# Attention scores of the plain dimensions as four float32r products in 64 rows, two heads side by side, with the maxima in a product of their own

## The chip, the core and the metric

The kernel runs on one core of one Trainium2 chip. The metric is the device time of one execution in microseconds, lower is better; a figure for a kernel is the median of its runs. Engines are named as in the profile: PE is TensorE (PEld its weight loads), DVE VectorE, ACT ScalarE, POOL GpSimd, SP the engine that here only issues DMAs.

## The reference, cut to what matters

The reference is a network of two layers over 1024 tokens of 256 numbers, each block with a layer norm ahead of it and a residual sum behind it. In order: attention a (16 heads of 16 dimensions), a ternary feed-forward block, attention b (a gated delta rule), the feed-forward block again, attention c (as a, with other weights), a mixture of experts, attention d (causal, 16 plain dimensions and 64 rotated ones for each head), the mixture of experts again. The change concerns the scores in a, c and d:

```python
# a and c, for each head; a adds a bonus per key
scores = q @ k.T * scale                # 16 dimensions
out = softmax(scores) @ v
# d
scores = (einsum('bhtd,bhsd->bhts', q, k) + einsum('bhtd,bsd->bhts', qr, kr)) * scale
scores = where(causal, scores, -inf)
out = softmax(scores) @ v
```

All is float32.

## The kernel before

**Blocks.** Everything stays on the chip: `x` (1024 tokens in eight tiles of 128) lives in SBUF and each block adds to it. `HALF` is 512 tokens, `P` 128, `GH` 4 heads make a group, `HT` 4 tiles a half, `NT` 8 tiles.

**The class `Stack` (L365 to L472)** holds q and k of the plain dimensions so that one product gives a nearly exact score. `make` takes 128 rows (8 heads by 16 dimensions) of q or k for 512 tokens from PSUM, copies them to `full`, and splits them into three bfloat16 pieces: ACT casts (L402), the engine named in `eng` subtracts (L403), ACT casts the rest (L405), POOL subtracts (L406). SP writes the pieces to a DRAM tile `dpc` (L407). `fetch` (L415) reads them back in another arrangement: for each head 96 rows, which are the six pairs of pieces that matter (`RUNS`), 16 dimensions each, in three DMAs. So a head's scores are one bfloat16 product over 96 rows. In the q block rows 96 to 98 hold the three pieces of the negated row maximum, and in the k block ones (L400), so that the transposed scores come out with the maximum already taken off, in a product over 99 rows (`rows`, L445).

**`attend` (L172 to L363)** runs with its order written out by hand. A unit is a group of four heads for one half of the queries; there are eight. A step `n` does three things, each for another unit or key tile:

- `look`: scores of one query tile against up to 512 keys, two heads into one double PSUM bank (tag `s`, two of them), and DVE's negated `reduce_max` over it (L227); in d DVE adds the causal mask first (L224).
- `weigh`, ten steps later (`LAG`): the same scores transposed, one key tile against up to 512 queries. Each head has a PSUM bank of tag `st`, of which there are three; ACT writes the exponential to `pr` (L252, in a with a bias L254). In d POOL cuts the diagonal block.
- `gather`, two steps after that: the sums over keys, four heads in four column strips of 32 into one bank (tag `o`, one of it), float32 (L279).

Within a step the order on PE is: two heads' looks and two heads' weights, the gather, then the same for the other two heads. `products` (L262) issues the matmuls: part by part, and within a part the two looks and then the two weights. In a and c `parts` is `[stack.rows]`, in d `[wide, stack.rows]`, where `wide` is the float32 product of the 64 rotated dimensions, heads in rows 0 to 63 and 64 to 127 by turns. In the first ten steps there are looks alone (four heads in one go), in the last ten weights alone (two heads in a double `s` bank, two in `st` banks), and at the end two steps of gathers.

When a unit's looks end, `settle` (L291) takes the smaller of the two negated maxima and `Stack.begin` (L454) splits it in three pieces on POOL; a step later `Stack.place` (L465) turns them with a product against the identity into a bank of tag `st`, DVE copies them (L470) and SP moves them into rows 96 to 98 of the q block (L472). When a unit's gathers end, `close` (L302) divides by the sums: DVE transposes (L311), POOL multiplies. `early`, `chores` and `last` are lists of further work put into given steps: the blocks of q and k still to be made, values, the output projection (L492, also in a bank of tag `st`), the next block's norm, loads.

**`plain`** (L500) prepares a and c, **`attn_d`** (L577) d: there the staging tiles of `make` are the later `pr` buffers and a spare tile. Outside `attend` a planner orders the instructions by costs and due times.

[...]

## Time and profile before

| what | value |
| --- | --- |
| median of three runs | 1514.51 us (1509.39 to 1522.26) |
| profiled execution | 1517.28 us, its span 1515.6 us |
| granted TensorE clock, mean | 0.957 |
| PE, PEld, DVE, ACT, POOL busy | 93%, 45%, 54%, 43%, 25% |
| attention a | 0 to 274 us |
| attention c | 615 to 862 us |
| attention d | 1013 to 1357 us |
| between them, and after d | feed-forward, b, feed-forward; mixture of experts |

The span is the time from the first to the last instruction of the profiled execution. In the profile's groups a line stands for all instructions of one source line with the same operands: number, busy time, mean time of one, and the idle time of the engine ahead of them with what ended it. L267 is the one matmul of `products`; its groups differ by the names `s` (looks) and `st` (weights; `stt` in a double bank), and by bf16 (`rows`) or f32 (`wide`). Matmul times hold the latency of the pipe, so the distance from one start to the next says more than a mean. A float32 product shows as two records, each of two passes; a float32r product shows as one record with the form f32. In the timeline consecutive instructions of one group are merged: start, time from the first start to the last end, count. The windows give, for a stretch, its length and then busy time and number of instructions for PE, PEld, DVE, ACT and POOL, the granted clock, the DMA engines' share and GB/s.

### The profile page before, as it was taken

Reading aid. Unit: us, or ns where it says so; the run is one execution under the profiler, and the core shown is the slowest. Engines: PE = TensorE matmul, PEld = TensorE weight load, DVE = VectorE, ACT = ScalarE, POOL = GpSimd, SP = SyncE. Lnnn points to the kernel's source line nnn. Section 1 sums busy time; section 2 is a strip of 40 time slices with the busy share of each in tenths; the row PEclk is TensorE's granted clock in tenths of the full one; section 3 lists DMA queues with packets and bytes.
Section 4 is the critical chain, followed back from the end, with each engine's and each line's share of the span. In section 5 each row is a group of like instructions: output and inputs, shape, how many; then the busy total and the mean of one; then the engine's idle time right before and its main releaser. Section 6 shows DMA issues by size and latency. Waiting matters only on the chain.

```text
span 1515.6 us, 18778 instructions
## 1 busy us (share of the span) xinstructions
PE 1402.0 (93%) x7250; PEld 679.8 (45%) x7250; DVE 824.8 (54%) x1357; ACT 645.1 (43%) x1165; POOL 373.0 (25%) x574
## 2 busy tenths in 40 slices
PE   5899989988799999899989999998899999899999
PEld 3222322665456888423332434553333334444454
DVE  4788768545673564688867231236545555523111
ACT  3488668445542235367756531112233333233100
POOL 1211100430458004211100124332221222230533
PEclk9799989998899999989999989999999999998999
DMA  5412002000012110531300100003310100000000
GB/s 157 111 33 87 2 1 71 0 1 0 9 34 53 28 40 1 140 82 30 105 15 1 61 1 0 0 2 109 81 33 0 32 2 2 1 1 1 0 14 14
DMA packets 51000, 51.40 MB, mean 34 GB/s; under 512 B 25116, under 2 KB 45212, under 8 KB 49436
## 3 DMA queue, kind: packets, MB, share of 16 engines
q1 hardware_dynamic: 42944, 35.82, 9.1%
q10 hardware_dynamic: 7968, 14.40, 3.8%
q8 instruction: 57, 0.93, 0.3%
q14 instruction: 31, 0.25, 0.1%
HBM read 37.06 MB, written 12.85 MB: 33 GB/s over the span
## 4 chain that ended last, share of the span: by engine, by line
PE 79%; DVE 11%; issue 3%; ACT 3%; DMA 2%; POOL 1%; ACTq 0%; SPq 0%; DVEq 0%; POOLq 0%
PE s L267 14%; PE st L267 11%; PE o L279 9%; DVE mx L227 4%; PE pu L1385 3%; PE po L1563 3%; PE pj L155 3%; PE pu L1507 3%; PE pg L1385 3%; PE pg L1507 3%; PE po L155 2%; PE py L1545 2%; PE ln L759 2%; PE pg L155 2%; PE pu L155 2%
## 5 line engine op out<-in xcount | busy, mean ns | idle before, releaser
L227 DVE TENSOR_REDUCE mx<-s 128x2 f32<-128x1024 f32 (+3 forms) x352 | 395.5, 1146 | 119.3 <-PE s L267 117.0
L252 ACT ACTIVATE pr<-st 128x512 f32<-128x512 f32 (+3 forms) x408 | 201.2, 556 | 214.7 <-PE st L267 211.5
L267 PE MATMUL s<-k,q 96*128 96x512 bf16 (+3 forms) x704 | 209.8, 386 | 14.3 <-DVE mx L227 12.7
L267 PE MATMUL st<-q,k 99*128 99x512 bf16 (+3 forms) x644 | 195.3, 377 | 5.7 <-ACT pr L254 2.4
L279 PE MATMUL o<-pr,V 128*32 128x512 f32 (+3 forms) x1408 | 182.0, 590 | 0.0
L254 ACT ACTIVATE pr<-st,bonus 128x512 f32<-128x512 f32 x236 | 145.3, 688 | 41.5 <-PE st L267 41.4
L267 PEld LDWEIGHTS <-q 96*128 96x128 bf16 x704 | 53.1, 99 | 203.6 <-issue 178.1
L267 PEld LDWEIGHTS <-k 99*128 99x128 bf16 x704 | 67.3, 100 | 93.0 <-issue 23.5
L1519 DVE TENSOR_TENSOR sl<-sl,pg 128x512 f32<-128x512 f32 (+1 forms) x48 | 30.8, 642 | 132.3 <-PE pg L1507 112.3
L267 PE MATMUL s<-kr,qr 64*128 64x512 f32 (+3 forms) x384 | 91.8, 540 | 4.2 <-DVE mx L227 2.2
L1514 ACT ACTIVATE sl<-pu 128x512 f32<-128x512 f32 (+1 forms) x48 | 26.8, 561 | 144.4 <-PE pu L1507 141.1
L1521 POOL TENSOR_TENSOR hT<-sl,mask 128x512 f32<-128x512 f32 x40 | 50.6, 1266 | 147.7 <-DVE sl L1519 98.1
L267 PE MATMUL st<-qr,kr 64*128 64x512 f32 (+3 forms) x344 | 78.1, 506 | 0.1
L313 POOL TENSOR_TENSOR raw<-raw,rc 128x512 f32<-128x512 f32 x24 | 25.1, 1047 | 187.9 <-DVE rc L312 187.9
L258 POOL TENSOR_SCALAR_AFFINE_SELECT pr<-pr 128x128 f32<-128x128 f32 x128 | 35.4, 292 | 124.8 <-ACT pr L252 123.6
L224 DVE TENSOR_TENSOR s<-s,squares 128x256 f32<-128x256 f32 x64 | 27.6, 431 | 69.8 <-PE s L267 69.6
L279 PEld LDWEIGHTS o<-pr,V 128*32 128x32 f32 x1408 | 29.1, 109 | 77.9 <-issue 73.1
L91 POOL TENSOR_TENSOR hT<-sl,hT 128x512 fp32r<-128x512 f32 x32 | 41.1, 1293 | 85.2 <-ACT hT L90 85.2
L267 PEld LDWEIGHTS s<-kr,qr 64*128 64x128 f32 x384 | 31.6, 186 | 51.7 <-issue 21.2
L135 PE MATMUL ln<-squares,xn 128*128 128x128 f32 x112 | 22.7, 303 | 34.1 <-DVE xn L132 31.5
L1385 PE MATMUL pu<-xT,m_up 128*128 128x512 f32 (+1 forms) x112 | 50.0, 597 | 0.0
L267 PEld LDWEIGHTS st<-qr,kr 64*128 64x128 f32 x344 | 36.9, 192 | 23.9 <-issue 14.1
(355 smaller groups left out, 2161.1 us busy)
## 6 DMA issues: line engine op xcount, KB each, us to landing
dpc<-pc SPq DMA_DIRECT2D x16, 384.0 KB
k<-dpc SPq DMA_DIRECT2D x12, 192.0 KB
k<-dpc ACTq DMA_DIRECT2D x6, 384.0 KB
q<-dpc SPq DMA_DIRECT2D x6, 384.0 KB
dpc<-spare SPq DMA_DIRECT2D x5, 384.0 KB
q<-dpc SPq DMA_DIRECT2D x12, 128.0 KB
k<-dpc SPq DMA_DIRECT2D x12, 128.0 KB
k<-dpc ACTq DMA_DIRECT2D x6, 256.0 KB
```

What stands on the lines that cost most here:

```text
L91: eng.tensor_tensor(dst[:, 1], src, dst[:, 0].bitcast(F32), ALU.subtract)
L155: pe.matmul(ps, lhsT=a, rhs=b, start=(n == 0), stop=(n == len(pairs) - 1))
L227: dve.reduce_max(maxima[u][:, pair : pair + 2, t % HT, c // HALF], ps[:, :, :size], axis=AX.X, negate=True)
L252: act.activation(pr[:, js, :wide], ps, AF.Exp)
L254: act.activation(pr[:, js, :wide], ps, AF.Exp, bias=bias[:, kt : kt + 1])
L258: pool.affine_select(block, block, [[1, P]], ALU.is_ge, 0.0, base=0, channel_multiplier=-1)
L267: pe.matmul(dst, lhsT=a, rhs=b, start=(i == 0), stop=(i == len(parts) - 1))
L279: pe.matmul(sums[u][32 * j : 32 * j + 32, c0:c1], lhsT=V[:, kt, 17 * (g * GH + j) : 17 * (g * GH + j) + 32], rhs=weights[m][0][:, j, c0 - ...
L1385: pe.matmul(ps[rs, own], lhsT=wt[wn][:, k, es], rhs=xT[:, k, tokens], start=(k == 0), stop=False)
L1507: pe.matmul(ps[rs, own], lhsT=wt[wn][:, es], rhs=z[hf, m, j][:, tokens.start - cols.start : tokens.stop - cols.start], start=False, stop=T ...
L1521: pool.tensor_tensor(hT[rs, own], sl[rs, own], masks[3 + j][rs, tokens], ALU.mult)
L1563: pe.matmul(po[b], lhsT=l, rhs=r, start=(n == 0), stop=False)
```

## The change

Each of q and k is split into two float32r pieces instead of three bfloat16 ones (`halve`), and a head's rows are 64 instead of 96: four products of pieces (q0k0, q0k1, q1k0, q1k1) of 16 dimensions each. Even heads of a group lie in rows 0 to 63 of the block, odd heads in rows 64 to 127; `across` orders the weights' columns to match. `fetch` makes four DMAs, of 32 rows each, that repeat pieces as the four products need.

The maxima leave the q and k blocks. They go to a tile `top` (bfloat16, cleared once), rows 0 to 11 and 64 to 75 (three pieces by four heads, twice), and a constant `pick16` selects the head: `shift` is a part of its own, a bfloat16 product over 64 rows that is issued only for the transposed scores, after all products of the part `rows`. `place` therefore issues two DMAs.

```diff
--- before.py
+++ after.py
@@ -262,9 +262,11 @@
         def products(todo):
             for i, part in enumerate(parts):
                 for dst, h, qs, ks, turn in todo:
+                    if part(h, qs, ks, turn) is None:
+                        continue
                     q, k = part(h, qs, ks, turn)
                     a, b = (k, q) if turn else (q, k)
-                    pe.matmul(dst, lhsT=a, rhs=b, start=(i == 0), stop=(i == len(parts) - 1))
+                    pe.matmul(dst, lhsT=a, rhs=b, start=(i == 0), stop=(i == len(parts) - 2 + turn))
 
         def gather(m, c0, c1):
 
@@ -369,9 +371,9 @@
 
 
 
-        RUNS = ((0, 0, 48), (48, 0, 32), (80, 0, 16)), ((0, 0, 48), (48, 16, 32), (80, 32, 16))
-        ROWS = 96
+
         BH = 8
+        ROWS = 64
 
         def __init__(self, p, dp, space=None):
 
@@ -381,30 +383,33 @@
                 self.stage = self.p.__enter__()
             self.of = {}
             self.kept = {}
+            self.tops = {}
+            self.pick = load(p, "pick16", w["pick16"], [P, 2, P])
+            self.ring = []
+            self.extend(p.tile([P, HALF], BF16, tag=f"top{n}", name="top") for n in range(1 if space else 2))
+
+        def extend(self, more):
+
+            for t in more:
+                pool.memset(t, 0.0)
+                self.ring.append(t)
 
         def make(self, n, b, hf, ps, use, eng):
 
             if self.space is None:
                 full = self.stage.tile([P, HALF], F32, tag="full", name="full", bufs=2)
-                rest = self.stage.tile([P, HALF], F32, tag="rest", name="rest", bufs=1)
-                pc = self.stage.tile([P, 3, HALF], BF16, tag="pc", name="pc", bufs=2)
+                pc = self.stage.tile([P, 2, HALF], F32R, tag="pc", name="pc", bufs=2)
             else:
                 flat = self.space()
-                full, rest = flat[:, :HALF], flat[:, HALF : 2 * HALF]
-                pc = flat[:, 2 * HALF : 2 * HALF + 3 * HALF // 2].bitcast(BF16).rearrange("p (c n) -> p c n", c=3)
-            d = self.dp.tile([3 * P, HALF], BF16, tag=f"d{n}{b}{hf}", name="dpc")
+                full = flat[:, :HALF]
+                pc = flat[:, HALF : 3 * HALF].bitcast(F32R).rearrange("p (c n) -> p c n", c=2)
+            d = self.dp.tile([2 * P, HALF], F32, tag=f"d{n}{b}{hf}", name="dpc")
             use(b, full, ps)
             name = "k" if n else "q"
-            st = self.of[n, b, hf] = self.blocks.tile([P, self.BH, HALF], BF16, tag=name, name=name, bufs=3 + n)
-            if n:
-                nc.sync.dma_start(out=st[self.ROWS : self.ROWS + 3], in_=w["ones16"])
-            first, last = (2, 0) if n else (0, 2)
-            act.copy(pc[:, first], full)
-            eng.tensor_tensor(rest, full, pc[:, first], ALU.subtract)
+            self.of[n, b, hf] = self.blocks.tile([P, self.BH // 2, HALF], F32R, tag=name, name=name, bufs=3 + n)
+            halve(eng, pc, full)
             yield
-            act.copy(pc[:, 1], rest)
-            pool.tensor_tensor(pc[:, last], rest, pc[:, 1], ALU.subtract)
-            nc.sync.dma_start(out=d.rearrange("(c p) n -> p c n", p=P), in_=pc)
+            nc.sync.dma_start(out=d.rearrange("(c p) n -> p c n", p=P), in_=pc.bitcast(F32))
             self.kept[n, b, hf] = d
             yield
 
@@ -414,9 +419,17 @@
 
         def fetch(self, n, b, hf, eng, hs=slice(0, BH)):
 
-            d = self.kept[n, b, hf].rearrange("(r h) n -> r h n", h=self.BH)
-            for dst, src, m in self.RUNS[n]:
-                eng.dma_start(out=self.of[n, b, hf][dst : dst + m, hs], in_=d[src : src + m, hs])
+
+            d = self.kept[n, b, hf].rearrange("(c s r j) n -> s c r j n", c=2, s=2, j=self.BH // 2)
+            js = slice(hs.start // 2, hs.stop // 2)
+            for side in range(2):
+                for m in range(2):
+                    src = d[side, m, None] if n == 0 else d[side]
+                    r = side * self.ROWS + m * self.ROWS // 2
+                    eng.dma_start(
+                        out=self.of[n, b, hf].bitcast(F32)[r : r + self.ROWS // 2, js],
+                        in_=src[:, :, js].to_broadcast([2, 16, js.stop - js.start, HALF]),
+                    )
 
         def rest(self, early, make, hf, later):
 
@@ -443,13 +456,21 @@
                 at(last + 4 + n, work)
 
         def rows(self, h, qs, ks, turn):
-            m = self.ROWS + 3 if turn else self.ROWS
+            r = slice(h % 2 * self.ROWS, (h % 2 + 1) * self.ROWS)
             return tuple(
                 self.of[n, h // self.BH, c.start // HALF][
-                    :m, h % self.BH, c.start % HALF : c.start % HALF + c.stop - c.start
+                    r, h % self.BH // 2, c.start % HALF : c.start % HALF + c.stop - c.start
                 ]
                 for n, c in ((0, qs), (1, ks))
             )
+
+        def shift(self, h, qs, ks, turn):
+
+            if not turn:
+                return None
+            r = slice(h % 2 * self.ROWS, (h % 2 + 1) * self.ROWS)
+            c0 = qs.start % HALF
+            return self.tops[h // GH, qs.start // HALF][r, c0 : c0 + qs.stop - qs.start], self.pick[r, h % GH // 2, :]
 
         def begin(self, ap, g, hf, nm):
 
@@ -468,8 +489,9 @@
             pe.matmul(pt, lhsT=self.kept.pop((g, hf)).rearrange("p c n -> p (c n)"), rhs=ident16, start=True, stop=True)
             nmT = ap.tile([3 * n, P], BF16, tag="nmT", name="nmT")
             dve.tensor_copy(nmT, pt)
-            j0 = g % 2 * GH
-            nc.sync.dma_start(out=self.of[0, g // 2, hf][self.ROWS : self.ROWS + 3, j0 : j0 + GH, :], in_=nmT)
+            top = self.tops[g, hf] = self.ring[len(self.tops) % len(self.ring)]
+            for side in range(2):
+                nc.sync.dma_start(out=top[side * self.ROWS : side * self.ROWS + 3 * GH], in_=nmT)
 
     def value_tile(p):
 
@@ -530,7 +552,7 @@
         early = {}
         stack.rest(early, make, 0, later)
         out_tile = partial(out_project, wt[letter + "_wo"], wt[letter + "_bo"])
-        attend(a2, pp, [stack.rows], stack, V, False, bias, early, out_tile, after, last)
+        attend(a2, pp, [stack.rows, stack.shift], stack, V, False, bias, early, out_tile, after, last)
 
     def attn_a(wt, norm, after, later, last):
 
@@ -687,9 +709,11 @@
                 for j in range(2):
                     early[(g + 2) * NT + LAG - NT + j].append(partial(turned_rows, g, 0, j))
             spare[0] = xpool.tile([P, KC * S], F32, tag="xT", name="spare")
+            more = [wt[n].rearrange("p k n -> p (k n)").bitcast(BF16) for n in ("d_wqd", "d_wkvd")]
+            early[0].append(lambda: stack.extend(more))
             stack.rest(early, make, 1, [])
             attend(
-                a2, pp, [wide, stack.rows], stack, V, True, None, early, partial(out_project, wo, None), after,
+                a2, pp, [wide, stack.rows, stack.shift], stack, V, True, None, early, partial(out_project, wo, None), after,
                 deque(),
             )
             ctx_d.close()
@@ -1732,7 +1756,9 @@
         "m_order": np.tile(np.arange(EXP, 0, -1), (P, 1)),
     }
     c32 = {k: np.ascontiguousarray(v, dtype=np.float32) for k, v in c32.items()}
-    c16 = {"ones16": np.ones((3, 8 * HALF), ml_dtypes.bfloat16)}
+    side, row = np.divmod(np.arange(P)[:, None, None], 64)
+    pick = (row < 12) & (row % 4 == 2 * np.arange(2)[:, None] + side) & (np.arange(P) >= 0)
+    c16 = {"pick16": pick.astype(ml_dtypes.bfloat16)}
     return {**c32, **c16, "m_spread": np.stack([np.asarray(s, np.float32) for s in spread], 1).astype(ml_dtypes.bfloat16)}
 
 
@@ -1747,7 +1773,7 @@
     a, b, c, d, m = "L0_attn_a_", "L0_attn_b_", "L1_attn_a_", "L1_attn_b_", "L1_ffn_"
     def across(wt):
 
-        return wt.reshape(-1, 2, NH // 2, 16).transpose(0, 1, 3, 2).reshape(-1, NH * 16)
+        return wt.reshape(-1, 2, NH // 4, 2, 16).transpose(0, 1, 3, 4, 2).reshape(-1, NH * 16)
 
     w = {"x": i[a + "hidden_states"].reshape(S, D)}
     for n in "qk":
```

## The prediction

> **What bounds the kernel now.** I read the head of the page first, then the attention's matmul groups, then the timeline of a few steps, and last the windows that show three steps at a time.
>
> ```profile
> span 1515.6 us, 18778 instructions
> PE 1402.0 (93%) x7250; PEld 679.8 (45%) x7250; DVE 824.8 (54%) x1357; ACT 645.1 (43%) x1165; POOL 373.0 (25%) x574
> ...
> L267 PE MATMUL s<-k,q 96*128 96x512 bf16 (+3 forms) x704 | 209.8, 386 | 14.3 <-DVE mx L227 12.7
> L267 PE MATMUL st<-q,k 99*128 99x512 bf16 (+3 forms) x644 | 195.3, 377 | 5.7 <-ACT pr L254 2.4
> ```
>
> PE looks full, and the products that the change touches (`s` and `st` of L267, bf16) are 405 of its 1402 us. That share says little: what counts is what ends one step of `attend`. One whole step of attention a, PE and then ACT:
>
> ```profile
> 150.64 0.60 PE L267 MATMUL st<-q,k 99*128 99x512 bf16 x2
> 151.08 0.59 PE L267 MATMUL s<-k,q 96*128 96x512 bf16 x2
> 151.51 0.66 PE L267 MATMUL st<-q,k 99*128 99x512 bf16 x2
> 152.10 1.06 PE L279 MATMUL o<-pr,V 128*32 128x512 f32 x8
> 153.10 0.39 PE L267 MATMUL s<-k,q 96*128 96x512 bf16 x1
> ...
> 151.06 2.42 ACT L254 ACTIVATE pr<-st,bonus 128x512 f32<-128x512 f32 x4 [0.48 <-PE st L267]
> 153.96 0.69 ACT L254 ACTIVATE pr<-st,bonus 128x512 f32<-128x512 f32 x1 [0.48 <-PE st L267]
> ```
>
> Call a step's four transposed products st1, st2 (before the gather, L279) and st3, st4 (after it), and their exponentials e1 to e4. They share three PSUM banks in turn, so st2 can't start before e3 of the step before has read its bank. The pair at 151.51 takes 0.66 where the pair at 150.64 takes 0.60: its second product came late. The loop: e3 starts at 151.06 and takes 0.69; st2 starts 0.04 later; 0.31 until the gather (0.22 of product, 0.09 of change of tile shape); gather 1.00; two s 0.44; st3 to the start of its exponential 0.42 (150.64 to 151.06). Sum 2.90, and the gathers stand 2.90 apart. Two things confirm it. In a step where `place` takes one of the banks, the loop runs through e4, one exponential later (0.58): 3.48 is what these steps take. In attention c the exponentials take 0.60 instead of 0.69 and stand 0.49 apart: the loop is 2.81, PE's own sum 2.83 and observed 2.83; with `place` 2.81+0.49=3.30, observed 3.30. So a and c sit on a round trip through PE and ACT that is as long as PE's own work. Three steps each of a, c, and attention d:
>
> ```profile
> 72.61:81.31 8.70, 8.70 (x49) 2.56 (x48) 6.84 (x6) 8.16 (x15) 2.31 (x2) 1.00 0.20 56
> ...
> 662.70:671.20 8.50, 8.50 (x49) 2.56 (x48) 6.81 (x6) 7.08 (x15) 2.31 (x2) 1.00 0.20 61
> 1143.75:1163.13 19.38, 19.38 (x101) 6.96 (x100) 10.27 (x16) 6.51 (x13) 2.99 (x3) 1.00 0.00 1
> ```
>
> In d (6.46 a step) ACT works 6.5 of 19.4 us: here PE's own work is the bound.
>
> **Prices of the new products.** No float32r product in 64 rows exists. Nearest are the ffn's float32r products over 128 rows, and d's float32 products in 64 rows:
>
> ```profile
> 295.97 1.07 PE L155 MATMUL pg<-xT,f_wg 128*128 128x512 f32 x4
> ...
> 286.18 0.72 PE L155 MATMUL pg<-xT,f_wg 128*128 128x512 f32 x2
> ...
> 1157.67 0.92 PE L267 MATMUL s<-kr,qr 64*128 64x384 f32 x4
> 1158.42 1.02 PE L267 MATMUL st<-qr,kr 64*128 64x512 f32 x4
> 1159.38 0.50 PE L267 MATMUL s<-k,q 96*128 96x384 bf16 x2
> ```
>
> Four float32r products take 1.07, the last 0.39 of it: 0.227 from start to start, against 0.216 in bf16. After a wait (286.18) two take 0.72, so the first spacing is 0.33: its weight load (188 ns a row, bf16 100) starts only with the product, and 0.11 of it shows. In d two heads in rows 0-63 and 64-127 run at once: four records, two passes for each head, in the time of two (1158.42 to 1159.38). I take a float32r pair at 0.23, or 0.33 after a wait or a change of shape; the shift pair (bf16, 64 rows, `pick` and `top`) at 0.22. Bounds: 0.23 if the pair overlaps and the load hides, 0.45 if the two heads follow each other. Between float32r and bf16 in one shape I take no gap: at 471.99 a 128*128 f32 follows a 128*128 bf16 after 0.22, the bare product.
>
> **Attentions a and c.** Removed per step: eight bf16 products (1.73). Added: four pairs (0.92) and two shift pairs (0.43). PE's own sum falls from 2.83 to about 2.6. But the shifts stand behind both st, and an exponential can start only after its shift. The loop afterwards: wake 0.05; st2 0.33 (it waits, so its load shows; st1 has run); second shift and change of shape 0.31; gather 1.00; s pair 0.33 (load after the change of shape); st pair 0.23; shift to exponential 0.42; exponential 0.69. Sum 3.36 in a, 3.27 in c. By the gathers' starts, 33 steps of 2.90 and 6 of 3.48 get 0.46 longer, 17.9; 33 of 2.83 and 6 of 3.30 get 0.44 longer, 17.2. Three steps with `close` (3.22 in a) go to 3.36: 0.4. If both loads hid, the loops would be 3.14 and 3.05 and these steps cost 18; if one more load showed, 8.6 more (78 x 0.11).
>
> Last ten steps (no s): the second st waits for the exponential of the first of the step before: 0.05, 0.33, 0.42, the double exponential (next start 1.00 later, 0.92 in c), 0.69 (0.60): 2.49 and 2.32 against 1.97 now, on 5 and 8 clean steps: 5.4. Steps with an output projection (4.56) are PE's own work, with more changes of shape: 0.1 by ten, 1. Together **+42**, from +24 to +50.
>
> [...]
>
> **Attention d.** The rows part is behind the wide float32 part. Now it costs a change of shape in (0.10), two s and two st in turn, a change back (0.09) and the wide load that then shows (0.11). Afterwards all parts use 64 rows. Per pair this saves 0.28 (0.30 less 0.02 for the slower float32r) plus the s term (two bf16 less one pair: 0.20 at 512 columns, 0.05 at 128); a pair with the gather behind it still pays the change, and saves 0.09 plus the s term. st gains nothing: two in turn become pair and shift. Over the 38 joint steps: 38 x 0.37 = 14.1, and the s terms by the looks' widths (128 to 512) add 11.5: 25.6. The bank loop takes part of this: at 512 columns it is 0.05+0.97+0.23+0.23+0.31+1.00+0.97+0.86+0.23+0.23+0.42+0.60=6.10 against PE's 5.98 (two pairs of 2.39, gather and change 1.09, a load 0.11), and with narrower s it falls less than PE does. I take three quarters, **-19** (bounds -13, -26), and -3 in the ten steps of looks (bounds -6, 0).
>
> **The rest.** `make` loses an ACT cast (0.62) and a POOL subtraction (1.16) in the chain before the first looks; its two pieces are a third more bytes to DRAM and back (512 for 384 KB), with a fourth fetch to issue (0.43). Later blocks stand behind DVE's reductions, 1.13 each. -1 per attention, **-3** (-6, +2). `place` issues two DMAs instead of one, 0.70 each on SP; only the second head of a pair waits for the second, and the gather covers most: **+1** (0, +8). Its DMA waits on SP for DVE's copy of `nmT`; in the looks the `dpc` writes and fetches stand behind it, and they have a step to spare. A `top` comes round after two units (three in d at first), when its shifts are long done. The `pick16` load and the clearing of `top` cost nothing: the norm and the projections hide them; uncovered, one SP issue (0.46 as b_wg's) per attention. Clock: with s pairs PE does less in the DVE-bound looks.
>
> ```profile
> 45.99:49.40 3.41, 1.99 (x9) 0.67 (x7) 2.93 (x3) 1.30 (x2) 1.40 (x2) 1.00 0.84 203
> 49.40:52.81 3.41, 2.56 (x7) 0.70 (x6) 3.41 (x4) 0.62 (x1) 0.64 (x1) 0.50 0.62 129
> ```
>
> A window with PE busy 1.99 of 3.41 precedes half clock. The looks will have more such windows, the steps of 3.36 will not (some 2.6 of work): **+2** (0, +8). [...]
>
> **Sum.** +42-19-3-3+1+2=+20, on the profiled execution's 1517.28 (span 1515.6): 1537. The median of the runs, 1514.51, is 2.8 lower, so 1535 is forecast. Differences within 1% (15 us) are about what a measurement here can't tell from none.
>
> **Rivals.** (A) The loads hide, as they do in a running stream: 78 x 0.22 in the loops and 13 x 0.11 in the last steps, 18 less: 1519, or 1516 as a median. For it: loads are issued far ahead in 295.97. Against: 286.18. (B) PE's work is the bound and the banks follow: a and c fall to DVE's 2.45 a step (two reductions of 1.22), 39 x 0.45 + 39 x 0.38 = 32 less; d the full 26+3, the start 3: 1453. It decides if the loop comes out under 2.45, that is, if st2 needn't wait for e3. For it: 93% PE, and c's ordinary steps fit PE's sum too. Against: 3.48, 3.30 and the 0.07 between a and c, which differ in ACT's work only. (C) The change doesn't do what it says: 64-row float32r pairs don't overlap. The loop gains 0.68 (s, st, shift), 57 us over 84 steps; d 38 x 1.34, 51: 1645. Against: d's float32 pairs.
>
> **Chances.** Forecast 0.60, A 0.20, B 0.14, C 0.06. Slower: nearly all of the forecast and C, 0.62; within 1%: A and the forecast's low edge, 0.22; faster: B and a little of A, 0.16. The forecast's own range, terms at their bounds but not all at once, is 1515 to 1570; with A it reaches down to 1502. B and C stay outside.
>
> **What would show it.** Gathers 3.36 apart in a, 3.27 in c, 5.8 in d's wide steps; PE waiting for ACT before st2; ACT with 0.9 idle a step; two s starts within 0.01; first spacing after a gather 0.33. Gathers at 2.45 would make the forecast wrong; at 3.1, A is right.

## The result, and the profile after

The changed kernel takes 1790.42 us (median of four runs, 1788.85 to 1792.27); the kernel before, on the same chip, 1518.38. The ratio is 1.180, with an interval from 1.173 to 1.187. The forecast was 1535 us, with a range up to 1570. The profiled execution has a span of 1787.5 us, 272 more than before. Here and below a median is of all runs of a kernel, while a ratio leaves out the few runs that were over 1.5% slower than the fastest of the same kernel.

The head of the page of the kernel after (busy time by engine), its chain by engine, and its groups for the products that the change touches. The chain is the work that ended last, followed back from the last instruction, at each step to what released it; DMA stands in it for a transfer, SPq and ACTq for the issuing of DMAs on SP and ACT, and the shares are of the span:

```profile
span 1787.5 us, 20323 instructions
PE 1444.6 (81%) x7954; PEld 752.6 (42%) x7954; DVE 824.8 (46%) x1357; ACT 640.8 (36%) x1141; POOL 351.3 (20%) x557
...
PE 63%; DMA 19%; DVE 6%; ACT 5%; issue 3%; SPq 2%; ACTq 1%; POOL 1%; DVEq 0%; POOLq 0%
...
L269 PE MATMUL s<-k,q 64*128 64x512 f32 (+3 forms) x704 | 223.0, 592 | 75.6 <-DMA k<-dpc 44.6
L269 PE MATMUL st<-q,k 64*128 64x512 f32 (+3 forms) x644 | 190.0, 420 | 56.5 <-ACT pr L254 30.0
L269 PE MATMUL st<-top,pick 64*128 64x512 bf16 (+2 forms) x544 | 151.9, 401 | 66.8 <-DMA top<-nmT 66.8
```

The chain by engine of the kernel before:

```profile
PE 79%; DVE 11%; issue 3%; ACT 3%; DMA 2%; POOL 1%; ACTq 0%; SPq 0%; DVEq 0%; POOLq 0%
```

PE is busy for 43 us more, and DMA has gone from 2% of the chain to 19%, from some 30 us to 340 in which a transfer is what the end waits for. Of the idle time ahead of the scores, 45 us end with a fetch of k and 67 with the maxima's DMA; the 30 us that end with ACT are the round trip over the banks that the prediction described. PE also runs slower: its mean granted clock is 0.889 where it was 0.957. The clock's records of both kernels hold only 1.0 and 0.5, in stretches of 3.41 us or whole multiples of it (but for the last), so (1-0.889) x 2 x 1787.5 gives 397 us at half clock, against 130 before. How much of the 272 us that alone is, no run separates. Some of the longest pieces of the chain from 30 to 175 us, in attention a, whose first gather stands at 133 (start, length, what):

```profile
30.78 16.99 DMA dpc<-pc
49.06 11.38 DMA k<-dpc
60.45 4.79 SPq L429
...
72.65 17.05 DMA dpc<-pc
93.70 24.97 DMA q<-dpc
121.21 4.63 ACTq L429
139.80 10.17 DMA dpc<-pc
152.73 22.65 DMA top<-nmT
```

`top<-nmT` moves two times 12 KB and takes 22.65 us: it isn't slow itself, it stands behind fetches (in experiment 2, where the fetches are faster, no such transfer has more than 4.94 us of the chain). SP and ACT each lose 4.6 to 4.8 us on one issue of a fetch (L429), where the prediction had 0.43. What the DMA engines do in this stretch (40 equal slices of 30 to 75 us; first the busy share of all 16 engines in tenths, then GB/s):

```profile
DMA  1117511111111111111111111111112111111111
GB/s 55 55 51 308 202 51 51 51 51 55 55 51 51 51 47 55 51 51 51 55 55 51 51 51 51 51 51 51 51 51 66 51 51 58 51 51 51 51 51 51
```

51 GB/s with a tenth of the engines busy, for nearly the whole of 45 us. In the packets of the trace a fetch comes as two streams side by side, 4096 bytes in 159 to 165 ns each, one packet behind the other: 2 x 4096 bytes in 160 ns are 51 GB/s, and two packets at a time are an eighth of 16 engines, as in the busy share (0.13 from 36 to 56 us). So a fetch of 1 MB takes 20 us, on 2 engines out of 16, while the others idle.

The steady steps are as forecast. A step of attention a of the kernel after, PE and ACT:

```profile
187.53 1.06 PE L281 MATMUL o<-pr,V 128*32 128x512 f32 x8
188.53 0.50 PE L269 MATMUL s<-k,q 64*128 64x512 f32 x2
188.87 0.40 PE L269 MATMUL st<-q,k 64*128 64x512 f32 x2
189.10 0.39 PE L269 MATMUL st<-top,pick 64*128 64x512 bf16 x2
...
189.53 2.61 ACT L254 ACTIVATE pr<-st,bonus 128x512 f32<-128x512 f32 x4 [0.78 <-PE st L269]
189.56 0.39 PE L269 MATMUL st<-q,k 64*128 64x512 f32 x1
190.27 0.50 PE L269 MATMUL st<-q,k 64*128 64x512 f32 x1 [0.31 <-ACT pr L254]
190.28 0.73 PE L269 MATMUL st<-top,pick 64*128 64x512 bf16 x2
190.93 1.07 PE L281 MATMUL o<-pr,V 128*32 128x512 f32 x8
```

Two heads of a pair run in the time of one (0.40 for x2). The second of the step's first st pair starts at 190.27 and waited for ACT; ACT idles 0.78. From gather to gather 3.40, forecast 3.36. Three steps of a and 10 us of c, by windows (length, busy time of PE, PEld, DVE, ACT, POOL, the clock, DMA share, GB/s):

```profile
180.76:190.93 10.17, 9.33 (x61) 3.37 (x60) 8.39 (x10) 7.60 (x13) 1.05 (x1) 1.00 0.01 2
921.90:931.90 10.00, 9.56 (x60) 3.52 (x60) 7.95 (x9) 6.76 (x13) 2.34 (x2) 1.00 0.16 56
```

10.17 are three steps of a; gathers in c stand 3.30 apart (forecast 3.27), in d's wide steps 5.78 to 6.05 (5.8).

By the starts of the first look, the first gather and the last gather of each attention, the span falls into these parts (us; the last two columns are two experiments below):

| part | before | after | 16-row fetches | dimensions swapped |
| --- | --- | --- | --- | --- |
| to a's first look | 32.9 | 41.5 | 30.7 | 31.6 |
| a: first look to first gather | 33.5 | 91.6 | 49.3 | 37.4 |
| a: gathers | 201.8 | 257.3 | 219.3 | 215.9 |
| to c's first look | 357.8 | 366.6 | 358.6 | 358.6 |
| c: first look to first gather | 32.2 | 89.0 | 42.5 | 38.0 |
| c: gathers | 192.9 | 248.2 | 211.7 | 215.3 |
| to d's first look | 186.7 | 183.1 | 181.8 | 183.2 |
| d: first look to first gather | 64.0 | 101.1 | 69.6 | 61.7 |
| d: gathers | 250.0 | 244.2 | 232.8 | 232.8 |
| to the end | 163.9 | 165.0 | 165.0 | 165.0 |

Of the 272 us, 152 are in the three stretches from first look to first gather. The gathers of a and c have 111 more. Most of that isn't in the steady steps: in a, two steps take 18.2 and 15.6 us, in the places where the chain has `top<-nmT` (22.65 us at 152.73 and 15.56 at 229.39).

### The profile page after: what moved, and what is told of

Read it like the earlier page. It is cut to its first block, busy times and chain, and to the rows that moved or that the text cites. A ratio compares the mean times of both kernels' runs of the same rounds, so it can differ in the third digit from the quotient of the medians.

```text
span 1787.5 us, 20323 instructions
## 1 busy us (share of the span) xinstructions
PE 1444.6 (81%) x7954; PEld 752.6 (42%) x7954; DVE 824.8 (46%) x1357; ACT 640.8 (36%) x1141; POOL 351.3 (20%) x557
## 4 chain that ended last, share of the span: by engine, by line
PE 63%; DMA 19%; DVE 6%; ACT 5%; issue 3%; SPq 2%; ACTq 1%; POOL 1%; DVEq 0%; POOLq 0%
PE st L269 12%; PE o L281 8%; PE s L269 7%; DMA dpc<-pc 5%; DMA top<-nmT 5%; DMA q<-dpc 5%; PE pu L1409 2%; PE po L1587 2%; PE pu L1531 2%; PE pg L1409 2%; PE po L155 2%; PE pg L1531 2%; PE pj L155 2%; PE py L1569 2%; SPq L429 2%
## 5 line engine op out<-in xcount | busy, mean ns | idle before, releaser
L269 PE MATMUL s<-k,q 64*128 64x512 f32 (+3 forms) x704 | 223.0, 592 | 75.6 <-DMA k<-dpc 44.6
L269 PE MATMUL st<-q,k 64*128 64x512 f32 (+3 forms) x644 | 190.0, 420 | 56.5 <-ACT pr L254 30.0
L269 PE MATMUL st<-top,pick 64*128 64x512 bf16 (+2 forms) x544 | 151.9, 401 | 66.8 <-DMA top<-nmT 66.8
L269 PEld LDWEIGHTS s<-k,q 64*128 64x128 f32 x704 | 81.8, 208 | 218.6 <-issue 96.2
L269 PEld LDWEIGHTS st<-q,k 64*128 64x128 f32 x644 | 90.1, 197 | 118.4 <-ACT pr L254 53.3
L269 PEld LDWEIGHTS <-pick 64*128 64x128 bf16 x704 | 46.5, 96 | 140.2 <-issue 137.1
L269 PE MATMUL s<-kr,qr 64*128 64x512 f32 (+3 forms) x384 | 97.5, 551 | 5.5 <-DVE mx L227 3.6
L269 PE MATMUL st<-qr,kr 64*128 64x512 f32 (+3 forms) x344 | 85.7, 516 | 0.3 <-ACT pr L252 0.3
L91 POOL TENSOR_TENSOR pc<-full,pc 128x512 fp32r<-128x512 f32 x10 | 12.7, 1274 | 237.8 <-ACT pc L90 237.8
L269 PEld LDWEIGHTS s<-kr,qr 64*128 64x128 f32 x384 | 37.2, 197 | 50.6 <-issue 20.5
```

The costliest lines, as they stand in the source:

```text
L91: eng.tensor_tensor(dst[:, 1], src, dst[:, 0].bitcast(F32), ALU.subtract)
L269: pe.matmul(dst, lhsT=a, rhs=b, start=(i == 0), stop=(i == len(parts) - 2 + turn))
```

## The experiments

**1. How many engines carry a fetch.** In the source of a changed fetch, `d[side]` broadcast to `[2, 16, heads, 512]`, the outermost dimension is 2. The first two runs issue each as two DMAs of 16 rows, in one case for all fetches, in the other for k's alone.

```diff
-                    src = d[side, m, None] if n == 0 else d[side]
-                    r = side * self.ROWS + m * self.ROWS // 2
-                    eng.dma_start(
-                        out=self.of[n, b, hf].bitcast(F32)[r : r + self.ROWS // 2, js],
-                        in_=src[:, :, js].to_broadcast([2, 16, js.stop - js.start, HALF]),
-                    )
+                    for c in range(2):
+                        r = side * self.ROWS + m * self.ROWS // 2 + c * 16
+                        eng.dma_start(
+                            out=self.of[n, b, hf].bitcast(F32)[r : r + 16, js],
+                            in_=d[side, m if n == 0 else c][:, js],
+                        )
```

> The changed kernel, with each fetch issued as eight DMAs of 16 partition rows instead of four whose source has an outermost dimension of 2. Bytes and products are the same. Theory (two engines): in the changed kernel's trace the packets of a fetch come two at a time, 4096 bytes in 159 ns, so a fetch of 1 MB is carried by 2 of 16 DMA engines and takes some 20 us, and the rest queues behind it. With 16 rows outermost the packets spread over 16 engines; a fetch takes 6 to 8 us, the waits for DMA fall from 19% of the chain to some 2%, and the time falls to what the prediction's other terms give, 1535, and some 5 more for four more issues a fetch: about 1540 (1520 to 1565). Rival (bytes: 4-byte pieces and every piece read twice from DRAM): nothing changes but the number of issues, 1780 or more. Rival (half of each: engines and bytes): 1600 to 1700. The steady loops stay: gathers 3.4 apart in attention a, 3.3 in c, 5.8 to 6.0 in d's wide steps.

> The changed kernel with only k's fetches in DMAs of 16 rows; q's keep the outermost dimension of 2. Half of the fetches are k's. Theory (two engines): a part of the excess goes with them, but the first looks need both a q and a k, and q's fetch takes 20 us by itself: the time lies between the changed kernel and the one with all fetches in 16 rows, 1600 to 1720. Rival (bytes): 1780 or more. If the time were near 1540, q's fetches would be hidden and k's alone the loss.

Measured: all fetches 1563.85 us, ratio 1.030 (1.024 to 1.035); k's alone 1704.83 in one run. So 226 of the 272 us go with the two engines, and the dose holds: with q's fetches left as they were, 71, 69 and 88 us lie between first look and first gather. DMA is down to 3% of the chain. That bytes or repeated reads were the loss is out: they are the same. Not as expected are 24 us that remain above 1540. The table has them: the stretch from first look to first gather is still 15.8, 10.3 and 5.6 us longer than before.

**2. The order of the dimensions alone.** One edit to the changed kernel: 16 outermost instead of 2. Since q's and k's rows change their order alike, the scores stay as they were. Four DMAs a fetch, same bytes.

```diff
-                    src = d[side, m, None] if n == 0 else d[side]
+                    src = d[side, m, :, None] if n == 0 else d[side].rearrange("c r j n -> r c j n")
...
-                        in_=src[:, :, js].to_broadcast([2, 16, js.stop - js.start, HALF]),
+                        in_=src[:, :, js].to_broadcast([16, 2, js.stop - js.start, HALF]),
```

> The changed kernel with one edit: in the source of a fetch the two outermost dimensions change places, 16 features by 2 pieces instead of 2 by 16 (the rows of a half side then alternate between the pieces, for q and k alike). Four DMAs a fetch, the same bytes, 32 rows each. Theory (the outermost dimension of the source sets how many DMA engines carry it, and the rest of the loss with 16-row fetches, 26 us, is their rate and number: 8192-byte packets of 974 ns to 16 neighbouring rows, against 309 ns to 128 rows, and eight issues for four): the packets spread over 16 engines, and the time comes to the prediction's own sum, 1541 (1530 to 1553), the stretch from first look to first gather within 6 us of the kernel before in each attention. Rival (the order of the dimensions doesn't matter, a DMA with a repeated or strided source is slow as such): 1780 or more. Rival (the loss of 26 us is not the fetches'): as with 16 rows, 1560 to 1570.

Measured: 1541.7 us (1540.61 to 1547.72), ratio 1.016 (1.010 to 1.022). The head of its chain, and its DMA engines in 40 slices of 36 to 56 us:

```profile
PE 79%; DVE 9%; ACT 6%; issue 4%; DMA 1%; POOL 1%; ACTq 0%; DVEq 0%; SPq 0%; POOLq 0%
...
DMA  6678765647656999999000000959999889999949
GB/s 172 221 205 229 221 213 189 197 172 238 205 139 246 328 356 414 377 377 336 33 25 29 25 25 4 246 147 295 262 246 246 197 180 180 262 229 262 197 98 262
```

Some 200 GB/s where the same four DMAs with the same bytes ran at 51. The cause of these 249 us (1790.4 less 1541.7) is settled: two dimensions in the wrong order. With 2 outermost the packets come two at a time, an eighth of 16 engines; with 16 outermost the share of all 16 is 0.6 or more in 29 of these 40 slices. What other sizes of that dimension do, this run doesn't show.

**3. What 16-row fetches lose.** In the run with 16-row fetches all 16 engines take part, yet between 56 and 75 us, where the packets of ACT's fetches take 92.5% of the engines' time, only 151 GB/s are moved. Here the pieces are written to DRAM twice, in the order of the tile's rows, and a fetch is one DMA of 128 rows.

```diff
+            to = d.rearrange("(s m c r) n -> s m c r n", s=2, m=2, c=2)
+            for side in range(2):
+                for copy in range(2):
+                    out = to[side, :, copy] if n == 0 else to[side, copy]
+                    nc.sync.dma_start(out=out.rearrange("c r n -> r c n"), in_=pc.bitcast(F32)[...])
...
+            d = self.kept[n, b, hf].rearrange("(p j) n -> p j n", j=self.BH // 2)
+            eng.dma_start(out=self.of[n, b, hf].bitcast(F32)[:, js], in_=d[:, js])
```

> The changed kernel, with the pieces written to DRAM twice, in the order of the tile's rows (four writes of 256 KB instead of one of 512 KB), so that a fetch is one DMA of 128 partition rows instead of eight of 16. Theory (what 16-row fetches still lose against the prediction, from the first look to the first gather 15.8, 10.3 and 5.6 us in a, c and d, is the time to issue eight DMAs a fetch, 0.46 to 0.56 each on SP and ACT): these stretches fall back to within 4 us of the kernel before each, and the time by 15 to 28 us to 1542 (1530 to 1552). Rival (bytes): twice the bytes written, so the stretches get longer and the time is 1565 or more. Rival (the wait is for the maxima's way through POOL, PE, DVE and DMA): no change, 1558 to 1568.

Measured: 1557.19 us, ratio 1.026 (1.020 to 1.031): 15 less was the least expected, and 7 came. The stretches did fall, to 37.3, 37.2 and 66.1 us, within 5.0 of the kernel before. But the parts ahead of the first looks grew by 6.7, 4.8 and 4.5 us against 16-row fetches. The chain says why, by line: with 16-row fetches from 14 to 50 us, then with ordered writes from 20 to 80.

```profile
by line: SPq L429 38.3%; PE pv L155 19.2%; DMA dpc<-pc 17.5%; PE pj L155 15.0%; issue 5.1%; ACT full L580 2.2%; ACT xT L73 2.1%; PE ln L135 1.9%; ACT pc L90 1.7%; DVE pc L91 1.4%; DVE xT L71 1.2%; DVE xn L132 0.9%; DVE V L512 0.4%; SPq L412
...
by line: DVE mx L227 23.2%; PE pj L155 15.8%; SPq L416 10.3%; DMA k<-dpc 9.4%; PE st L269 8.8%; PE s L269 8.6%; DMA top<-nmT 7.4%; DMA dpc<-pc 7.2%; ACT pr L254 3.5%; PE o L281 2.6%; issue 1.6%; DVE pc L91 1.2%; ACT pc L90 1.0%; DVE nmT L49
```

In the first, the end waits for SP to issue fetches (L429), as the theory had it. In the second that is gone; now SP's issues of the writes (L416, eight of 0.61 to 1.24 ahead of the first look) are on the chain, so the gain is real (12.0, 5.3 and 3.5, together 20.8), and its price, 16, eats three quarters of it. Swapping the dimensions has the gain without the price. Beside the number there is the rate. The DMA engines while fetches run, to 16 rows in 56 to 75 us and to 128 rows in 60 to 75:

```profile
DMA  9997949291974989996979969595959596969696
GB/s 121 121 155 86 190 52 224 35 224 17 190 86 48 155 280 435 479 280 77 188 77 128 148 86 190 69 207 69 207 69 207 69 173 86 190 86 190 86 190 86
...
DMA  9999979659689896510963899996000000000000
GB/s 388 410 410 306 295 164 202 120 153 208 235 322 388 360 464 243 192 55 29 224 131 109 350 415 437 415 437 284 22 0 0 0 0 0 0 0 0 0 0 0
```

In the right half of the first pair, where ACT's fetches go to 16 rows each, the share is 0.9 and 0.5 or 0.6 by turns at 190 and 86, or 207 and 69, GB/s: 138 in the mean. Fetches to 128 rows: 388 to 437. In the packets, 8192 bytes take 974 ns (median, 58 to 80 us) when they go to 16 neighbouring rows and 309 when they go to 128. So here the rate rose with the rows that a transfer reaches: 138 GB/s for 16, 207 for 32 (experiment 2, the mean of the slices from 48 to 56 us), 388 to 437 for 128. What makes it so no run shows.

**4. The round trip over three banks.** With 16-row fetches, the gather is cut into halves, one after each pair.

```diff
                         if v is not None:
-                            if pair == 0:
-                                gather(v, 0, HALF)
+                            gather(v, pair * HALF // 4, (pair + 2) * HALF // 4)
```

> The changed kernel with 16-row fetches, and the gather of a step cut into two halves of 256 columns, one after the first pair of scores and one after the second. Nothing else moves. Theory (round trip over three PSUM banks): each half of the gather lies in another lap of the banks, so a lap has 0.50 less: 3.36-0.50=2.86 in a, 2.77 in c, though PE has two more changes of shape (0.2) a step; over 78 steps some 38 us less than with 16-row fetches alone, about 1525 (1515 to 1540). Rival (PE's own work is the bound in these loops): the gathers stand 3.5 apart or more and the time is 10 us or more above that of 16-row fetches alone.

Measured: 1551.79 us, ratio 1.022 (1.016 to 1.028), 12 less than with the gather whole. PE of this kernel in one half step of a, and ACT:

```profile
88.82 0.50 PE L269 MATMUL s<-k,q 64*128 64x512 f32 x2
89.16 0.40 PE L269 MATMUL st<-q,k 64*128 64x512 f32 x2
89.40 0.39 PE L269 MATMUL st<-top,pick 64*128 64x512 bf16 x2
89.72 0.64 PE L281 MATMUL o<-pr,V 128*32 128x256 f32 x8
89.82 1.27 ACT L254 ACTIVATE pr<-st,bonus 128x512 f32<-128x512 f32 x2 [0.42 <-PE st L269]
90.28 0.50 PE L269 MATMUL s<-k,q 64*128 64x512 f32 x2
```

In this half step the wait for ACT is gone, and it takes 0.34+0.24+0.32+0.56=1.46. A step, which is two half steps, falls from 3.39 to 2.96 to 3.03 in a (mostly 3.03) and from 3.30 to 2.94 in c, though PE has more to do. PE's own work would have made it longer: that rival is out, the loop was the bound. Both fall by some 0.36, where 0.50 was expected. In c two half steps of 1.47 are PE's own sum of 1.46, so there PE is probably the bound after the cut. In a every other half step is mostly 1.55 to 1.57, and the 0.09 between 3.03 and 2.94 is again the difference of the exponentials (0.69 and 0.60), so ACT still seems to count there; no run settles it. Of the 38 us expected, the gathers of a and c give back 12.3 and 7.7; steps with an output projection got longer (4.71 whole, 1.56+3.39 cut), and d, where PE is the bound, spans 3.7 more.

**5. The maxima in the rows.** The product of the maxima stands between a st and its exponential. Here 48 rows hold three products of pieces, without q1k1, and rows 48 to 50 the maxima against ones.

```diff
+        PAIRS = (0, 0, 1), (0, 1, 0)
...
+                for m, c in enumerate(self.PAIRS[n]):
+                    r = side * self.ROWS + m * 16
+                    eng.dma_start(out=self.of[n, b, hf].bitcast(F32)[r : r + 16, js], in_=d[side, c][:, js])
...
-        attend(a2, pp, [stack.rows, stack.shift], stack, V, False, bias, early, out_tile, after, last)
+        attend(a2, pp, [stack.rows], stack, V, False, bias, early, out_tile, after, last)
```

> Fetches in 16 rows, and no shift product: three products of pieces in 48 rows (the product of the two lower pieces is left out) and the maxima in three more rows of the same product, against rows of ones, so that a st is one float32r pair. Theory (three PSUM banks in a round trip with the exponentials): the loop loses the shift of the second pair (0.22) and the st before the shift (0.23): 0.05+0.33+0.09+1.00+0.33+0.42+0.69=2.91 in a, 2.82 in c, as before the change; d keeps what the change brings there, and its loop of banks falls too, to 5.65 at 512 columns: 15 to 45 us below the kernel before, about 1480. Rival (PE's own work is the bound): the gathers stand 2.5 or less apart in a and c, the time is 1450 or less. Rival (16-row fetches don't mend the loads): 1650 or more.

Measured: 1502.42 us, ratio 0.990 (0.986 to 0.994). The loops are what the bank theory gives: 2.93 in a, 2.84 in c, where 2.91 and 2.82 were expected. The time is 22 above: 16-row fetches still cost 8.5 and 5.9 us ahead of the first gathers, and the gathers of a and c span 4.1 and 2.6 more than before although the loops are as short.

**6. When PE is no longer the bound: the clock.** With the gather in halves as well, the loop falls under DVE's two reductions. The first run adds the cut of experiment 4 to the kernel of experiment 5; the second also writes the pieces in the order of the rows and fetches 48 rows at a time. Both, like the two after them, leave out q1k1.

```diff
+            to = d.rearrange("(s m r) n -> s r m n", s=2, m=3)
+            for side in range(2):
+                src = pc.bitcast(F32)[side * self.ROWS : (side + 1) * self.ROWS]
+                two = src if n else src[:, :1].to_broadcast([self.ROWS, 2, HALF])
+                nc.sync.dma_start(out=to[side, :, :2], in_=two)
+                nc.sync.dma_start(out=to[side, :, 2], in_=src[:, self.PAIRS[n][2]])
```

> Three products of pieces in 48 rows and the maxima in three rows of the same product (the product of the two lower pieces is left out), 16-row fetches, and the gather cut into two halves as well. Theory (banks): a lap of 2.91 loses 0.50 and comes under PE's own sum (four pairs 0.23, gather 1.00, four changes of shape 0.09, two to four loads 0.11: 2.5 to 2.7): steps of 2.6 in a and c instead of 2.94, 78 x 0.34 = 26 less than with the gather whole: 1475 (1465 to 1490). Rival (PE is the bound already at 2.94): the steps get longer, 1510 or more.

> Three products of pieces in 48 rows and the maxima in three rows of the same product (the product of the two lower pieces is left out), the gather in two halves, and the pieces written to DRAM in the order of the rows (four writes), so that a fetch is two DMAs of 48 rows. If both theories hold (banks, and issues at the start), their gains add: 1475 less 10 to 20: 1460 (1445 to 1475), some 3.5% under the kernel before. If the issues don't matter, it is as the one with 16-row fetches.

Measured: 1521.33 (ratio 1.001, 0.997 to 1.005) and 1511.54 (0.994, 0.990 to 0.998): 46 and 52 above what was expected, though the half steps are 1.24 to 1.28, DVE's reduction of 1.23, shorter than I had them. What is missing is about what the clock costs. Mean clock and span of the second are 0.915 and 1510.1; (1-0.915) x 2 x 1510.1 gives 257 us at half clock, against 130 before the change. An estimate: where a half step takes 2.16 instead of 1.24, the 127 us more cost 127 x (1-1.24/2.16), 54 us. Windows of 3.41 us around a fall of the clock:

```profile
143.68:147.10 3.42, 2.99 (x32) 1.36 (x33) 3.33 (x5) 3.42 (x6) 0.00 (x0) 1.00 0.43 108
147.10:150.51 3.41, 2.01 (x22) 0.75 (x19) 2.25 (x4) 1.97 (x4) 1.05 (x1) 1.00 0.72 290
150.51:153.92 3.41, 3.41 (x24) 0.92 (x22) 2.83 (x3) 1.75 (x3) 0.00 (x0) 0.50 0.00 0
208.54:211.95 3.41, 1.49 (x18) 0.66 (x14) 2.37 (x6) 1.44 (x4) 1.07 (x1) 1.00 0.00 0
```

The last row is the window ahead of another fall. PE and DVE around the first, and PE in the window of the last row:

```profile
148.20 0.64 PE L279 MATMUL o<-pr,V 128*32 128x256 f32 x8
148.36 0.71 DVE L314 STREAM_TRANSPOSE O<-raw 128x512 f32<-128x512 f32 x1 [1.16 <-POOL raw L313]
...
150.24 0.58 PE L267 MATMUL s<-k,q 48*128 48x512 f32 x2 [1.40 <-DVE mx L227]
...
153.33 1.08 PE L279 MATMUL o<-pr,V 128*32 128x256 f32 x8
...
155.49 1.08 PE L279 MATMUL o<-pr,V 128*32 128x256 f32 x8
...
210.69 0.41 PE L135 MATMUL ln<-squares,xn 128*128 128x128 f32 x2 [1.92 <-DVE xn L132]
```

`close` keeps DVE from its reductions, PE waits 1.40 for a free s bank, and a window with PE busy 2.01 of 3.41 is followed by half clock, in which a half step takes 2.16. This stretch lasts 10 us. In the window of the last row PE waits 1.92 for DVE's part of the next block's norm, and the stretch behind it lasts 27. No threshold in PE's busy time comes out of these windows: in the same run one with 1.97 (1314.50 to 1317.91) is followed by full clock, and one with 2.52 (259.70 to 263.11) by half. Now give PE useless work in these places: three repeats of the first st products in the two steps behind a `close`, and each look's s products three times in the steps that only look; then, in another run, one repeat behind a `close` and nothing else.

```diff
+                        if n in behind:
+                            fill(todo[2:], 3)
                         products(todo)
```

> As the kernel with three products, the gather in two halves and two fetches of 48 rows (1510), with useless products added on PE in attentions a and c: in the steps behind the end of a unit the first float32r products of st are made four times instead of once before the look's, and in the steps that only look each s three times. Theory (clock): that kernel's windows of 3.41 us with PE busy under 0.6 or so stand where DVE empties the sums, and each costs 2 to 8 windows at half clock, in which a step takes 4.32 instead of 2.48 (259 us at half clock against 130 before the change). With more work on PE in these places the clock stays, and more work makes the kernel faster: 1465 (1445 to 1490). Rival (the half clock has another cause): the same number of steps at 4.32 and the time 1510 or more.

> As the kernel with three products, the gather in two halves and two fetches of 48 rows (1510), with one useless repeat of the first st products in the two steps behind the end of a unit in a and c, and none elsewhere. In the kernel with three repeats the clock stayed full there, but each filled half step took 2.06 instead of 1.24 to 1.78, so that the gain was spent. Theory (clock, and the size of the filler): one repeat lifts the windows of 0.59 to about 0.7, costs 5 us in all and saves the stretches at half clock that begin there: 1495 (1480 to 1507). Rival (0.7 is not enough, or the half clock begins elsewhere): 1508 or more.

Measured: 1520.96 (ratio 1.004, 1.001 to 1.006) and 1507.65 (0.987, 0.981 to 0.993). The window behind a `close` with one repeat:

```profile
99.60:103.02 3.42, 2.94 (x21) 1.28 (x21) 3.28 (x4) 1.86 (x4) 0.00 (x0) 1.00 0.00 0
```

2.94 busy, and the clock stays: in attention a it holds from 76 to 195 us without a break, with three repeats from 77 to 200, where it fell at 150.5 without them. So more work in these places did keep the clock there. As a gain it comes to little. Three repeats make a half step of 2.06 out of 1.24 to 1.78, which costs what the clock gives. One repeat lies 4 us under the kernel without it, and their intervals overlap: no verdict. In the second half of a and c the clock still falls, where the next block's norm and the output projections keep DVE from the looks; some 240 us at half clock are left ((1-0.921) x 2 x 1510.5 with one repeat).

**7. The change where PE is the bound.** Attention d alone, first as changed (with 16-row fetches), then with three products and the maxima in rows (q1k1 left out in d), then its pieces also written as in the diff of experiment 6. `Stack` is the class of the kernel before, `Stack2` that of each variant.

```diff
-            stack = Stack(a1, dp, space)
+            stack = Stack2(a1, dp, space)
...
-                a2, pp, [wide, stack.rows], stack, V, True, None, early, partial(out_project, wo, None), after,
+                a2, pp, [wide, stack.rows, stack.shift], stack, V, True, None, early, partial(out_project, wo, None), after,
```

The second edit is the first run's; with the maxima in the rows the line stays as it was.

> Attentions a and c as in the kernel before (bf16 pieces in 96 rows, maxima in the same product), attention d as changed (float32r pieces in 64 rows, two heads side by side, maxima in a product of their own), its fetches in 16 rows. Theory (the prediction's terms: d gains 19 in its joint steps and 3 in its looks, a and c lose 42): 20 us below the kernel before, 1495 (1485 to 1505), gathers 5.8 to 6.0 apart in d's wide steps against 6.46. Rival (d's saving is eaten by its bank loop and its starts): within 5 us of the kernel before.

> Attentions a and c as in the kernel before. Attention d with three float32r products of pieces in 48 rows and the maxima in three rows of the same product (the product of the two lower pieces is left out), two heads side by side, 16-row fetches. Theory (stages add): d's gathers span 220 us where the kernel before has 250, as they did when all three attentions were so, and a and c stay at 202 and 193: 30 to 40 us under the kernel before, 1478 (1470 to 1490). Rival (a faster d lowers the clock, or its start eats the gain): 1495 or more.

> Attentions a and c as in the kernel before; attention d with three float32r products of pieces in 48 rows and the maxima in rows (the product of the two lower pieces is left out), and its pieces written to DRAM in the order of the tile's rows, so that a fetch is two DMAs of 48 rows instead of six of 16. Theory (issues): in d the stretch from the first look to the first gather is 57.8 us with such fetches where it is 64.6 with 16-row ones: 3 to 7 us less, 1477 (1470 to 1482). Rival (the writes, four for one, cost as much): 1482 or more.

Measured: 1506.26 (ratio 0.993, 0.989 to 0.996), 1482.39 (0.978, 0.975 to 0.981) and 1478.96 (0.974, 0.971 to 0.978). The first gains 8 of 20: d's gathers span 232.9 instead of 250.0, as forecast, but 16-row fetches put 5.5 back ahead of its first gather. The last is 2.6% faster than the kernel before and beats both kernels; of its 40 us, d's gathers give 29.7 (220.3 against 250.0) and its looks 6.2 (57.8 against 64.0). In it PE stays the bound in d, in these 10 us at full clock:

```profile
1101.00:1111.00 10.00, 10.00 (x63) 4.84 (x61) 4.72 (x6) 3.51 (x8) 1.75 (x6) 1.00 0.44 85
```

Its wide steps take 5.39 where they took 6.45 before. Whether the ordered writes bring 3 us of this can't be told: the intervals of the last two touch.

## Why the prediction was wrong, and where it was right

**The step that failed** is "The rest", in its sentence on `make`: "its two pieces are a third more bytes to DRAM and back (512 for 384 KB), with a fourth fetch to issue (0.43)", **-3** with bounds -6 and +2. A fetch was priced by its bytes and its issue, as if the DMA engines came along in any number. In place of the -3 the runs put some +249 us (1790.4 against 1541.7), all of it in how many engines carry the fetch: with the two outermost dimensions swapped and nothing else, the changed kernel takes 1541.7, and the sum in the prediction was 1537, the forecast 1535. A warning stood in the prediction's own fence: in 45.99:49.40 the last two columns are a DMA share of 0.84 and 203 GB/s. I read that row for its clock. A stage whose DMA engines are that full has no room for a transfer on an eighth of the engines, at a quarter of that rate (51 GB/s), and a diff that changes a DMA's shape asks for its engines first.

**The other terms**, measured on the kernel with the dimensions swapped, whose span is 23.8 above before; the sum was 20:

| term | forecast | measured |
| --- | --- | --- |
| a and c, gathers | +42 | +14.1 and +22.5 = +36.6 |
| d, joint steps | -19 | -17.2 |
| d, looks | -3 | -2.3 |
| start and `make` (the parts ahead of the first looks) | -3 | -1.2+0.8-3.5 = -3.9 |
| looks of a and c (`place` +1, clock +2 lie here) | +3 | +3.9+5.8 = +9.7 |
| to the end | 0 | +1.1 |

- The loop is 3.39 and 3.30 (forecast 3.36 and 3.27), the last steps 2.57 and 2.39 (2.49 and 2.32). The steps with `place` got only 0.18 longer in a (3.66 against 3.48) and 0.36 in c (3.66 against 3.30), where 0.46 and 0.44 were added: 6 x 0.28 + 6 x 0.08 = 2.2 of the 5.4 that a and c cost less; where the other 3.2 lie stays open.
- Experiments 4 and 5 show the loop to be what the prediction said, the banks and not PE: rival B is out, and rival A with it, since its 3.14 was not seen. The pairs overlap, so rival C is out too.
- The looks of a and c cost 9.7 where 3 were entered. In c the maxima's DMA takes 4.94 us of the chain there, so `place`, entered as +1 with an upper bound of +8, was probably sized too small; how much of the 9.7 is its own no run tells.
- That d gains is confirmed (experiment 7). Three quarters of the 25.6 that PE saves there was a choice; 17.2 of it arrived, so how near the -19 came is partly luck.
- It is luck too that the sum is only 4 off (20 against 23.8): the gathers of a and c cost 5.4 less than forecast and their looks 6.7 more, and the two nearly cancel.

## What to carry to other kernels

Before a DMA is priced by its bytes, look at the outermost dimension of its source and at how many partitions it reaches; here the same four DMAs ran at 51 or at 200 GB/s by the order of two dimensions, and that was some 250 us out of 272, and 8192 bytes took 974 ns to 16 rows and 309 to 128. A product between a score and its exponential costs its own time and also lengthens the round trip over the banks (a step of a took 3.39 with it, 2.93 with the maxima in the rows); count how long one lap takes before counting PE's work. Where PE is relieved until another engine is the bound, expect the clock to fall in some of the places where that engine pauses (257 us at half clock in experiment 6, 130 before), and put the saving where PE stays full, as in d (10.00 of 10 us at a clock of 1.00).

## What the runs showed of the hardware that I had not expected

- A DMA with 2 outermost in its source ran on 2 of 16 engines at 51 GB/s, and a transfer of 24 KB behind such fetches stood for 22.65 us on the chain; with 16 outermost, the same bytes at some 200 GB/s.
- Packets to 16 neighbouring rows took 92.5% of the time of all 16 engines while 151 GB/s were moved (8192 bytes in 974 ns); to 128 rows it was 388 to 437 (309 ns). A full DMA share is not a full rate.
- One window of 3.41 us with PE busy 2.01 was followed by 10 us at half clock, one with 1.49 by 27 us; the longest wait of PE in them was 1.40 and 1.92 us. With less work on PE, the kernel of experiment 6 spent 257 us at half clock where the kernel before spent 130.
